# Moving layer 1's sums into step 7, beside the products of heads 0 to 3, and the maximum of head 5 ahead of the residual

## The chip, the cores and the metric

The kernel runs on one core of a Trainium2 chip. A core has five engines with their own instruction queues, each of which works strictly in order: PE multiplies matrices (its weight loads, PEld, overlap the products), DVE and ACT work on whole tiles, POOL works on tiles in SBUF and issues DMAs, and SP issues DMAs. PE writes its results to PSUM, a memory of eight banks, from where DVE and ACT read them. The metric is the time of one execution on the device in microseconds (us); lower is better.

## The reference, cut to what matters

Sixteen graphs of 1024 nodes with 256 features go through two layers, each with a norm ahead and a residual behind.

```python
# layer 0: attention with 8 heads of 32, masked by the graph
h = maximum(layernorm(x), 0)
Q, K, V = proj(Wq, bq), proj(Wk, bk), proj(Wv, bv)
scores = where(adj == 0, -inf, Q @ K.T * SCALE)
x = x + (softmax(scores) @ V) @ Wo.T + bo
# layer 1: edge scores from the features themselves
h = maximum(layernorm(x), 0)
e_k = leaky_relu((h * a_k) @ h.T, 0.2)        # one for each kind k = 1..4 of edge
scores = where(adj == k, e_k, -9e15)
x = x + softmax(scores) @ h
```

In these inputs adj holds only 0 and 1, so that one kind of edge occurs; a branch behind the loop handles the others and is not taken.

## The kernel before, in words

A tile is 128 nodes of a graph; there are 8 tiles to a graph and 128 in all. The main loop (L839) runs over s, one tile a round, and inside it over h = 0 to 7, which the text calls steps. The order of the instructions is written out by hand (`tc.manual_schedule()`, L787): each engine runs its share in the order of the source, and waits are put in where data or buffers require them. In one round several tiles are in work at different stages:

- `now` (class `Attend`) is the tile whose eight heads are scored. In step h PE makes `scores(h)` (L461), DVE takes the maximum and applies the mask (`softmax_max`, L473), and ACT does the exponential of the head before (`softmax_exp`, L490). The head before that is transposed: heads 0, 1, 4 and 5 by DVE in blocks that SP's DMAs then place (L381, L386), heads 2, 3, 6 and 7 by PE with copies by ACT (`turn_half`, L590, L591). Tile 7 of a graph has only heads 0 and 1 in blocks, tile 0 only heads 4 and 5; the others of heads 0, 1, 4 and 5 then go over PE with copies by DVE, and their exponentials write in another order.
- `now.combine(0)` (L526) multiplies heads 0 to 3 with the values in step 7; `was.combine(1)`, of the tile before, does heads 4 to 7 in step 3. `was.output()` (L541) writes y in step 4, `was.residual()` (L547) adds x on DVE in step 5, and `norms` (L182, L183, then POOL L167 to L172) takes the statistics of that and of the next piece.
- `piece` (class `Piece`) is a tile nine rounds ahead whose keys, queries and values are made: `normed` (ACT L223, step 4), `turn` (two PE transposes, L237, step 5), `turned` (two ACT copies, L249 and L250, step 5), `project(0, ...)` (k's projection, PE L267, step 6), `raised(0)` (ACT L309, step 7); in the next round, as `piece_was`, `project(1, ...)` in step 1, `values` in step 2, `raised(1)` (L309) in step 4.
- `edge` (class `Edges`) is a tile of layer 1, nine rounds behind: `score` in steps 0 and 2 (L627, L633), `softmax_max` in step 3 (L656), then `bend`, `leak` and, in step 6, `softmax_exp` (L680). In the next round, as `edge_was`, it is turned in blocks in step 0, and `gather(0)` and `gather(1)` (PE L698, 32 matmuls each) make its sums in steps 5 and 6. `store` (DVE L705, L707, and SP's output DMA L708) follows in step 6.

Rounds s = 0 to 9 have no gather, and rounds from s = 119 on have no `piece`.

Matmuls of combine and gather use a quarter of PE's columns each (128*32 in the profile), four side by side; all others use 128*128.

PSUM: `sides` hold the scores; of a tile in the middle, heads 4 and 6 and layer 1's edges have `sides[1]`, the others `sides[0]`. Two banks are cut in halves:

```python
banks = [ps_acc.tile([P, 2, D], F32, tag=f"acc{i}", name=f"acc{i}", bufs=1) for i in range(2)]
sums_place, brief, early, late = (banks[i // 2][:, i % 2, :] for i in range(4))
```

`sums_place` takes combine's products and layer 1's sums; `early` the projection of q; `late` the values, y, the piece's transposes and the projection of k, one after the other. All of them are called acc in the profile.

Behind the main loop the eight tiles of layer 1 of the last graph run by themselves; their sums alternate between `sums_place` and `late`.

Of the kernel before, what the change touches and what calls it, by code (L numbers as in the profile page):

```python
# [30 lines left out]
def by_blocks(t):  # L31
    return BY_BLOCKS.get(t, MIXED)
# [15 lines left out]
def gnn_kernel(  # L48
# [46 lines left out]
    sums_place, brief, early, late = (banks[i // 2][:, i % 2, :] for i in range(4))  # L95
# [92 lines left out]
    class Piece:  # L188
# [5 lines left out]
        def __init__(self, b, first, n=1):  # L194
            self.b, self.first, self.n = b, first, n
            self.cols = slice(first * P, (first + n) * P)
            self.projected, self.halved, self.queries = [], [], []
            self.tags = ("xin", "h0", "hT", "halves", "hTm") if n == 1 else ("pT", "pT", "pT", "p", "blocks")
# [158 lines left out]
    def load_key(b, h):  # L357
        kt = keys.tile([P, N], F32R, tag=f"k{h}", name=f"k{h}_{b}")
        c, r = divmod(h, GROUP)
        nc.sync.dma_start(  # L360
            out=kt.bitcast(F32),
            in_=kds[b][c, r * HD : (r + 1) * HD]
            .rearrange("d w n -> (d w) n").unsqueeze(1).to_broadcast([2 * HD, 2, N]),
        )
        keysets.setdefault(b, {})[h] = kt
# [228 lines left out]
    class Edges:  # L594


        def __init__(self, b, t, last=False):
            self.b, self.t, self.last = b, t, last
            self.rows = slice(t * P, (t + 1) * P)
            self.side = sides[t % 2 if last else 1]  # L600
            self.tags = {"sel": ("p", 4), "pT1": ("pT", 7)} if last else {}
            if last and t % 2:
                self.tags |= {"ha": ("hT", 1), "x1b": ("x1", 1), "h0": ("xb", 1)}
            self.sums = late if last and t % 2 else sums_place

        def buffer(self, tag, shape):
            tag, bufs = self.tags.get(tag, (tag, 1))
# [168 lines left out]
    def attend_of(s):  # L776
        return Attend(*divmod(s, NT)) if 0 <= s < B * NT else None

    def edges_of(s):
        s -= LAG  # L780
        return Edges(*divmod(s, NT), s >= (B - 1) * NT) if 0 <= s < B * NT else None

    def piece_of(s):
        s += LEAD
        return Piece(*divmod(s, NT)) if s < B * NT else None

    with tc.manual_schedule():  # L787
        first = [Piece(0, 0, 4), Piece(0, 4, 4)]
        piece_was, piece_next = Piece(1, 0), piece_of(0)
        now, nxt = attend_of(0), attend_of(1)  # L790
# [39 lines left out]
        piece, edge, edge_was = piece_next, None, None  # L830
# [8 lines left out]
        for s in range(B * NT + 1):  # L839
            b, t = divmod(s, NT)  # L840

            def load_keys(h, end):
                if t == NT - 1 and b + 1 < B and 2 * h + end in KEY_STEPS:
                    load_key(b + 1, KEY_STEPS.index(2 * h + end))
                if t == 0 and 0 < b < B and 2 * (HEADS + h) + end in KEY_STEPS:
                    load_key(b, KEY_STEPS.index(2 * (HEADS + h) + end))

            nxt2, edge_nxt, piece_nxt = attend_of(s + 2), edges_of(s + 1), piece_of(s + 1)
            for h in range(HEADS):
                ending, eh = (now, h - 1) if h >= 1 else (was, HEADS - 1)  # L850
                turning, th = (now, h - 2) if h >= 2 else (was, HEADS + h - 2)

                load_keys(h, 0)


                if now:
                    now.scores(h)
                if h == 0 and piece_was:
                    piece_was.halve(0)
                if s == 0 and h == 1:  # L860
                    first[1].values()
                if h == 3 and edge:
                    edge.softmax_max()
                if h == 5:
                    if was:
                        was.residual()
                    norms(was, piece_nxt)
                if h == 6 and edge_was:
                    edge_was.gather(1)
                if now:  # L870
                    now.softmax_max(h)
                if h == 6 and edge_was:
                    edge_was.store()


                if h == 1 and edge:
                    edge.keep(0)
                if h == 2 and gone:
                    gone.turned_normed()
                if ending:  # L880
                    ending.softmax_exp(eh)

                if h == 3 and was:
                    was.turned_reciprocals()
                if h == 3 and edge:
                    edge.bend()
                    edge.keep(1)


                if h == 3:  # L890
                    if was:
                        was.combine(1)
                    if piece_was:
                        piece_was.biased()
                    if was:
                        was.combined()
                if turning and th in by_blocks(turning.t):
                    turning.turn_blocks(th)
                    turning.place_blocks(th)
                elif turning:  # L900
                    turning.turn(th, 0)
                    turning.turn(th, 1)


                if h == 0:
                    if edge:
                        edge.score(0)
                    if gone:
                        gone.normed()
                    if edge_was:  # L910
                        edge_was.turn_blocks()
                        edge_was.place_blocks()
                if h == 1:
                    if gone:
                        gone.turn_normed()
                    if piece_was:
                        piece_was.project(1, 0)
                        piece_was.project(1, 1)
                    if was:
                        was.reciprocals()  # L920
                    if piece_nxt:
                        piece_nxt.load()
                if h == 2:
                    if edge:
                        edge.score(1)
                    if piece_was:
                        piece_was.values()
                    if was:
                        was.turn_reciprocals()
                        was.add_bias()  # L930
                if h == 3:
                    if nxt:
                        nxt.load_queries()
                    if edge:
                        edge.leak()
                    if edge_was:
                        edge_was.load_nodes()
                    if nxt:
                        nxt.flag()
                        nxt.mask()  # L940
                if h == 4:
                    if was:
                        was.output()
                    if piece_was:
                        piece_was.raised(1)
                        piece_was.halve(1)
                    if piece:
                        piece.normed()
                    if piece_was:
                        piece_was.write_queries()  # L950
                    if edge_nxt:
                        edge_nxt.prepare()
                    if nxt2:
                        nxt2.load()
                if h == 5:
                    if edge_was:
                        edge_was.gather(0)
                    if piece:
                        piece.turn()
                    if piece:  # L960
                        piece.turned()
                if h == 6:
                    if edge:
                        edge.softmax_exp()
                    if was:
                        was.keep()
                    if now:
                        now.load_nodes()
                    if piece:
                        piece.project(0, 0)  # L970
                        piece.project(0, 1)
                if h == 7:
                    if now:
                        now.combine(0)
                    if piece:
                        piece.raised(0)
                load_keys(h, 1)
            gone, was, now, nxt = was, now, nxt, nxt2
            edge_was, edge = edge, edge_nxt
            piece_was, piece = piece, piece_nxt  # L980
# [84 lines left out]
```

## Time and profile before

| what | before |
|---|---|
| median of three runs | 3070.12 us (3068.62 to 3073.23) |
| the profiled execution, its own time | 3076.4 us |
| its span in the profile | 3074.5 us |
| DVE busy, share of the span | 2515.6 us, 82% |
| ACT busy | 2654.5 us, 86% |
| POOL busy | 2177.6 us, 71% |
| gathers, PE L698 | 8192 matmuls of 382 ns, 496.9 us of PE's time |
| combines, PE L526 | 16384 matmuls of 275 ns, 533.4 us |
| scores, PE L461 | 2048 matmuls of 453 ns, 760.6 us |
| maxima, DVE L473 | 1024 of 1208 ns |
| exponentials, ACT L490 | 1024 of 1224 ns |

How to read the profile: the page gives the busy time of each engine and its share of the span. The list of waits says who stood idle, until whose instruction ended: total, times, longest. The view of windows gives, for a stretch of time, its length and then each engine's busy time. The timeline lists instructions in order of time: start, duration, engine, line, operation, output<-inputs, tile and count of merged instructions, and in brackets idle time ahead of them. Matmuls are pipelined: a group's duration reaches over the start of the next group, so the time between two starts is what the first costs PE.

### The profile page before, as it was taken

The numbers are of one execution on the slowest core, as the hardware profiler recorded it, in microseconds if no ns is written. First come the engines' busy times: TensorE is split into PE (matmuls) and PEld (weight loads), VectorE is DVE, ScalarE is ACT, GpSimd is POOL, SyncE is SP. The second block draws the span as 40 slices with busy tenths as digits, with TensorE's granted clock in tenths as the row PEclk, the third lists the DMA queues.
The fourth block names the chain that finished last, engine by engine and source line by source line (L and its number), as shares of the span: only waits on it lengthen the run. The fifth ranks groups of instructions, "written<-read, shape, count | busy, mean of one in ns | idle before, by whom it ended". The sixth has DMA issues, their size and how long they took to land. (4 is left out here: it accounts for less than half of the span.)

```text
span 3074.5 us, 96254 instructions
## 1 busy us (share of the span) xinstructions
PE 2965.6 (96%) x36722; PEld 2230.1 (73%) x36722; DVE 2515.6 (82%) x4453; ACT 2654.5 (86%) x5159; POOL 2177.6 (71%) x2999
## 2 busy tenths in 40 slices
PE   7889999999999999999999999999999999999998
PEld 5667777777777777777777777777777777776664
DVE  5878888888888888888888788888888888888885
ACT  5888888899898998889889888988989888898882
POOL 3657777777777777777777777777777777776542
PEclk9999999999999999999999999999999999999999
DMA  7766777877777786777777777787777777777653
GB/s 245 219 219 205 237 235 222 255 216 243 231 225 243 230 257 209 232 247 220 246 230 228 235 232 243 221 255 221 220 247 228 251 211 235 237 227 236 191 168 100
DMA packets 597828, 695.68 MB, mean 226 GB/s; under 512 B 63280, under 2 KB 528560, under 8 KB 597360
## 3 DMA queue, kind: packets, MB, share of 16 engines
q1 hardware_dynamic: 528288, 477.29, 51.9%
q0 software_dynamic: 66960, 210.04, 21.0%
q8 instruction: 295, 4.83, 0.7%
q10 hardware_dynamic: 2112, 2.10, 0.2%
q14 instruction: 173, 1.42, 0.1%
HBM read 252.98 MB, written 134.22 MB: 126 GB/s over the span
## 5 line engine op out<-in xcount | busy, mean ns | idle before, releaser
L473 DVE CUSTOM_DVE_ANT_0 p<-s,neg 128x1024 f32<-128x1024 f32 x1024 | 1236.2, 1208 | 220.7 <-PE s L461 185.1
L490 ACT ACTIVATE p<-p,nmx 128x1024 f32<-128x1024 f32 x1024 | 1249.4, 1224 | 132.5 <-DVE nmx L473 123.9
L461 PE MATMUL s<-k,qt 128*128 128x512 f32 x2048 | 760.6, 453 | 15.5 <-DVE nmx L473 4.3
L591 ACT COPY pT<-trp 128x512 f32<-128x512 f32 x1024 | 549.4, 590 | 95.3 <-PE trp L590 94.9
L590 PE MATMUL trp<-ident,p 128*128 128x128 f32 x4608 | 604.5, 274 | 4.7 <-ACT pT L591 1.5
L590 PEld LDWEIGHTS trp<-ident,p 128*128 128x128 f32 x4608 | 531.0, 140 | 104.0 <-ACT pT L591 10.8
L381 DVE STREAM_TRANSPOSE blocks<-p 128x1024 f32<-128x1024 f32 x456 | 564.5, 1238 | 12.3 <-ACT p L680 10.6
L526 PE MATMUL acc<-pT,v 128*32 128x128 f32 x16384 | 533.4, 275 | 41.8 <-ACT recT L520 30.0
L526 PEld LDWEIGHTS acc<-pT,v 128*32 128x32 f32 x16384 | 453.5, 110 | 153.0 <-ACT recT L520 85.0
L698 PE MATMUL acc<-h,pT 128*32 128x256 f32 x8192 | 496.9, 382 | 2.8 <-DVE h L707 1.7
L441 POOL TENSOR_SCALAR neg<-adj 128x1024 bf16<-128x1024 int32 x128 | 467.9, 3655 | 42.9 <-ACT neg L453 33.7
L461 PEld LDWEIGHTS s<-k,qt 128*128 128x128 f32 x2048 | 322.9, 191 | 106.3 <-issue 43.0
L698 PEld LDWEIGHTS acc<-h,pT 128*32 128x32 f32 x8192 | 241.8, 109 | 207.8 <-issue 65.6
L676 POOL TENSOR_TENSOR sel<-sel,less 128x1024 f32<-128x1024 f32 x120 | 286.8, 2390 | 68.9 <-ACT less L665 47.6
L633 PE MATMUL s<-h1T,ha 128*128 128x512 f32 (+2 forms) x744 | 272.8, 490 | 2.7 <-ACT h1T L569 1.6
L674 POOL TENSOR_SCALAR less<-top 128x1 f32<-128x1 f32 x120 | 31.9, 266 | 274.0 <-DVE top L656 273.9
L324 POOL DMA_DIRECT2D qd<-halves x240 | 177.5, 780 | 58.7 <-POOL halves L314 31.8
L490 ACT ACTIVATION_READ_ACCUMULATOR p<-p,nmx 128x1 f32 x1024 | 206.8, 202 | 0.0
L510 POOL COPY wide<-rec 128x256 f32<-128x256 f32 x128 | 53.8, 420 | 204.2 <-DVE rec L508 204.2
L330 POOL DMA_DIRECT2D kd<-halves x240 | 172.2, 766 | 35.5 <-POOL halves L314 35.4
L314 POOL TENSOR_TENSOR halves<-full,halves 128x256 fp32r<-128x256 f32 x240 | 176.8, 737 | 20.6
L633 PEld LDWEIGHTS s<-h1T,ha 128*128 128x128 f32 x744 | 126.7, 190 | 70.7 <-issue 45.0
(117 smaller groups left out, 4328.4 us busy)
## 6 DMA issues: line engine op xcount, KB each, us to landing
pT<-blocks SPq DMA_DIRECT2D x2304, 128.0 KB, 3.5
qt<-qd SPq DMA_DIRECT2D x128, 512.0 KB, 4.5
k<-kd SPq DMA_DIRECT2D x128, 512.0 KB, 7.3
adj<-in_adj POOLq DMA_DIRECT2D x127, 512.0 KB, 5.0
qd<-halves POOLq DMA_DIRECT2D x240, 256.0 KB, 2.7
kd<-halves POOLq DMA_DIRECT2D x240, 128.0 KB, 4.1
xb<-in_x POOLq DMA_DIRECT2D x128, 128.0 KB, 4.2
x1d<-x SPq DMA_DIRECT2D x128, 128.0 KB, 4.0
```

The costliest lines, as they stand in the source:

```text
L324: nc.gpsimd.dma_start(out=qds[self.b][self.first, oc].rearrange("p u w n -> p u (w n)"), in_=halves.unsqueeze(1).to_broadcast([P, 2, 2 * P]),)
L381: nc.vector.transpose(blocks.rearrange("p b j q -> p j b q"), p)
L441: nc.gpsimd.tensor_scalar(self.neg, self.adj, 0.0, MASKED, ALU.is_equal, ALU.mult)
L461: nc.tensor.matmul(self.ps[:, cols], lhsT=self.qt[:, h, :], rhs=keysets[self.b][h][:, cols], start=True, stop=True,)
L473: nc.vector.tensor_tensor_reduce(out=p, in0=sides[h in self.second], in1=self.neg, scale=-SCALE, scalar=FLOOR, op0=ALU.add, op1=ALU.min, a ...
L490: nc.scalar.activation(to, of, AF.Exp, bias=nmx, scale=-1.0, accum_out=self.sums[:, h : h + 1])
L526: nc.tensor.matmul(sums_place[r * HD : (r + 1) * HD, g * P : (g + 1) * P], lhsT=vs[self.b][:, j, place_of(h) : place_of(h) + HD], rhs=self ...
L590: nc.tensor.transpose(tr[:, j, :], p[:, jj * P : (jj + 1) * P], ident)
L591: copy(pT[:, half * 4 : half * 4 + 4, :], tr)
L633: nc.tensor.matmul(self.side[:, cols], lhsT=self.ha[:, c, :], rhs=h1T[:, c, cols], start=(c == 0), stop=(c == NC - 1),)
L676: nc.gpsimd.tensor_tensor(self.sel, self.sel, self.less, ALU.subtract)
L698: nc.tensor.matmul(self.sums[a * HD : (a + 1) * HD, :], lhsT=self.pT[:, j, a], rhs=h1s[self.b][:, j, :], start=(j == 0), stop=(j == NT - 1),)
```

## The change

In step 5 the maximum of head 5 stands ahead of `was.residual()` and `norms` in DVE's order. In step 6 `edge_was.gather(1)`, `store` and the projection of k are gone, in step 5 `gather(0)`. In step 7, behind `scores(7)` and the turning of head 5, now stand in this order: the projection of k, `gather(0)`, `gather(1)`, `store`, `combine(0)`, `raised(0)`. Layer 1's sums of all graphs but the last go to `early` in place of `sums_place`; those of the last graph stay where they were.

```diff
-            self.sums = late if last and t % 2 else sums_place
+            self.sums = (late if t % 2 else sums_place) if last else early
...
                 if h == 3 and edge:
                     edge.softmax_max()
+                if now:
+                    now.softmax_max(h)
                 if h == 5:
                     if was:
                         was.residual()
                     norms(was, piece_nxt)
-                if h == 6 and edge_was:
-                    edge_was.gather(1)
-                if now:
-                    now.softmax_max(h)
-                if h == 6 and edge_was:
-                    edge_was.store()
...
                 if h == 5:
-                    if edge_was:
-                        edge_was.gather(0)
                     if piece:
                         piece.turn()
                     if piece:
...
                     if now:
                         now.load_nodes()
+                if h == 7:
                     if piece:
                         piece.project(0, 0)
                         piece.project(0, 1)
-                if h == 7:
+                    if edge_was:
+                        edge_was.gather(0)
+                        edge_was.gather(1)
+                        edge_was.store()
                     if now:
                         now.combine(0)
                     if piece:
```

## The prediction

> **What bounds the kernel now.** I read the page first, then the waits of PE, then the busy time of one whole round (the loop body for one tile `now`, from `scores(4)` to the next `scores(4)`), then that round in order of time.
>
> ```profile
> PE 2965.6 (96%) x36722; PEld 2230.1 (73%) x36722; DVE 2515.6 (82%) x4453; ACT 2654.5 (86%) x5159; POOL 2177.6 (71%) x2999
> ```
>
> ```profile
> PE acc L526 <- ACT recT L520: 30.0, 43, 1.6
> PE acc L267 <- ACT hTm L250: 16.1, 10, 1.7
> ```
>
> ```profile
> 1571.04:1593.77 22.73, 22.73 (x288) 17.32 (x285) 19.41 (x34) 20.59 (x42) 17.53 (x25) 1.00 0.77 227
> ```
>
> PE is 96% busy, its longest wait adds up to only 30.0 us, and in the round from 1571.04 to 1593.77 (tile t = 2 into t = 3) it is busy for all 22.73 us (the second number). So PE sets the end, and a round costs what PE's queue costs. But DVE (19.41) and ACT (20.59) are close behind, in a strict order, so PE is full only because its own order has always something ready. That order is what the change touches. Steps 5 to 7 of that round, and what PE's neighbours do there:
>
> ```profile
> 1573.16 0.82 PE L461 MATMUL s<-k,qt 128*128 128x512 f32 x2
> 1573.81 1.04 PE L590 MATMUL trp<-ident,p 128*128 128x128 f32 x8
> 1574.78 1.93 PE L698 MATMUL acc<-h,pT 128*32 128x256 f32 x32
> 1576.64 0.44 PE L237 MATMUL acc<-ident,h 128*128 128x128 f32 x2
> 1576.84 0.71 PE L461 MATMUL s<-k,qt 128*128 128x512 f32 x2
> 1577.48 1.93 PE L698 MATMUL acc<-h,pT 128*32 128x256 f32 x32
> 1579.35 1.16 PE L267 MATMUL acc<-hT,wkT 128*128 128x128 f32 x8
> 1580.26 0.71 PE L461 MATMUL s<-k,qt 128*128 128x512 f32 x2
> 1580.90 1.95 PE L526 MATMUL acc<-pT,v 128*32 128x128 f32 x64
> 1582.78 0.73 PE L461 MATMUL s<-k,qt 128*128 128x512 f32 x2
> ```
>
> ```profile
> 1576.04 1.08 ACT L591 COPY pT<-trp 128x512 f32<-128x512 f32 x2
> ...
> 1577.12 0.38 ACT L249 COPY hT<-acc 128x256 f32<-128x256 f32 x1
> ...
> 1577.39 0.38 ACT L250 COPY hTm<-acc 128x256 f32<-128x256 f32 x1
> ```
>
> On PE: scores(5), transposes of head 3, gather(0), `piece.turn` (L237), scores(6), gather(1), k's projection (L267), scores(7), combine(0), scores(0) of the next round. A group costs PE the time to the start of the next group. The two gathers (1.86 and 1.87 us) stand where they fill PE while residual (DVE L547, 0.42 us from 1574.63) frees `late` and ACT copies `hT` and `hTm` out of it until 1577.77.
>
> **What the change removes on PE.** Gather and combine use 128*32 tiles, all around them 128*128. Entering such an island costs 0.07 to 0.10: eight transposes take 0.97 before gather(0) and 0.87 elsewhere (1571.61 to 1572.48), a score pair 0.64 instead of 0.57. Leaving costs about 0.1: the last gather matmul starts at 1576.33 (end less the 0.38 of one), a round of four takes 0.22, so its slot ends at 1576.55, and the next group starts at 1576.64. Three islands become one: two entries (0.17) and two exits (0.20) go, and the merged block is 1.86 + 1.87 + 1.88 - 0.20 = **5.41 us** from the first gather matmul to scores(0). The bound from below zero gain is 5.61 (no exit saved); I take 5.41, since the drain shows in the rows. No instruction is added or removed.
>
> **What it uncovers.** New PE order: scores(5), transposes of head 3, `piece.turn`, scores(6), scores(7), projection, block, scores(0). Two waits come up that gather(0) and gather(1) covered.
>
> *First, `piece.turn` writes `late`, which residual must have read.* The maximum of head 5 now stands ahead of residual on DVE: scores end at 1573.98, the maximum runs from 1574.02 and lets its successor start 1.15 later (as L473 does throughout), residual takes 0.42 from 1575.17 and ends at 1575.60. PE would be free at 1574.68; `piece.turn` starts at 1575.65, **0.97 us** idle. Then 0.20, scores(6) at 1575.85, scores(7) at 1576.42 (the maximum of head 5 is long there), PE free at 1576.99. Behind the waiting transposes stand both scores, but DVE is still in the norms (1.55 us after residual's start) until about 1576.8, so nobody else loses.
>
> *Second, the projection reads `hT`, and `late` must be copied out.* ACT runs without a gap from exp(3) through copies, `raised(1)`, `normed`, exp(4) and copies to `hTm`; none of it moves. It can only lose its wait for `piece.turn`: "ACT hT <- PE acc L237" is 12.1 us in 41 rounds. Against the first rounds, where the pair of copies is followed by `hTm`'s end 1.62 us after its start (141.83 to 143.45), this round could end 0.11 earlier, those of t = 0 and 1 0.41; over the rounds 0.23 on average. So `hTm` ends at 1577.54 on average instead of 1577.77, and PE waits about another 0.6 us.
>
> The trace has this case already. In the first ten rounds there is no layer 1, so no gather covers anything:
>
> ```profile
> 143.04 0.41 ACT L250 COPY hTm<-acc 128x256 f32<-128x256 f32 x1
> 143.50 1.16 PE L267 MATMUL acc<-hT,wkT 128*128 128x128 f32 x8 [1.65 <-ACT hTm L250]
> 144.41 0.70 PE L461 MATMUL s<-k,qt 128*128 128x512 f32 x2
> ```
>
> PE idles 1.65 us there; these are the 10 waits, 16.1 us, of the list above.
>
> **Sum of one round.** From the end of `hTm`: 0.05 to the projection, 0.91 for it (143.50 to 144.41, after a wait), 0.10 entry, 5.41 block = 6.47 to scores(0). Before it was 1582.78 - 1577.77 = 5.01. With `hTm` 0.23 earlier: 6.47 - 5.01 - 0.23 = **+1.23 us**; with 5.61 for the block +1.43, with the better exit of 0.13 each +1.17. From scores(0) on, every step keeps its order, PE is full again, so nothing gives the time back.
>
> *Tile t = 7 of each graph.* There heads 4 and 5 are turned on PE, head 5 right before the projection, and their exponentials are the 2.26 us kind:
>
> ```profile
> 1505.28 2.26 ACT L490 ACTIVATE p<-p,nmx 128x1024 f32<-128x1024 f32 x1
> ...
> 1511.57 0.73 PE L461 MATMUL s<-k,qt 128*128 128x512 f32 x2
> ```
>
> That exponential ends at 1507.54 and is bound by ACT's queue. After: 0.05, eight transposes 0.87, projection 0.81, entry 0.10, block 5.41 = 1514.78 instead of 1511.57, **+3.2 us** (scores(7) and gather(1) no longer fill the time).
>
> *Other edits.* `store` now reads `early` on DVE after the block's gathers, about 1.6 us ahead of scores(0), and `raised(0)` on ACT reads `late` in the same bank: 1574.63 for residual is 0.09 after `raised(1)` (1573.90 + 0.64) ended, though the two read different halves of that bank, so `raised(0)` will wait for `store`. ACT idles some 1.9 us, exp(7) behind it ends about 0.8 us after scores(0) starts; before it ended at 1583.58, also 0.8 after. Its next readers come later, so the cost is 0; without that cover up to 0.5 us a round. The Trainium skill, page "PSUM — Partial Sum Buffer", section "PSUM bank collisions raise a hardware error", says that two engines must be kept apart on one bank and quadrant even at other addresses, reads against reads included. It speaks against putting the sums beside `late`, and agrees with the 0.09; by it ACT must wait, without it ACT would go on at once, and both give PE the same sum here. The output DMA of `store` is issued about 1.7 us later against scores(0); behind it on SP stand the DMAs of layer 1's next tile, whose blocks DVE makes only after max(0). The x1 DMA and head 5's four placing DMAs now go ahead of it. POOL's norm runs at 1581.77, five us after its statistics, so their delay of half a us costs nothing.
>
> **Count.** Of 109 rounds with both a gather and a piece (s = 10 to 118), 13 have t = 7: 96 x 1.23 = 118, 13 x 3.2 = 42. The ten rounds without gather gain, since scores(7) now goes into the wait: from `hTm` to scores(0) 3.48 before, 0.05 + 0.91 + 0.10 + 1.88 = 2.94 after, -5. The nine last (no piece, no wait) gain some 0.4 each, -3. Sum +152, on the profiled execution's own 3076.4 us (span 3074.5) 3228; the median of the runs shown is 6.3 lower, so **3222 us**, 5% slower.
>
> **Rivals.**
> 1. *Faster: one island, waits covered elsewhere.* PE gains 0.37 plus 0.10 of the projection's slow start in 119 rounds: 3070 - 56 = 3014. For it stands that PE is the bound. The deciding point: scores(0) comes no later than before only if the projection starts by 1582.78 - 5.41 - 0.10 - 0.91 = 1576.36; PE is free for it only at 1576.99, even were `hTm` ready at once. Both waits would have to shrink to 0.4 us together.
> 2. *Only residual's wait stays,* ACT running earlier than its order lets me see: 1576.99 + 6.42 = 1583.41, +0.63 a round: 3070 + 69 = 3139.
> 3. *Typical rounds as forecast, t = 7 no worse than they:* 3222 - 13 x 2 = 3196.
> 4. *ACT's wait for `store` enters the chain* through exp(7) and the copies of head 6: +0.5 more in 109 rounds, 3277.
> 5. *No effect:* if the islands' gain met the waits, 3070.
>
> **Numbers.** Forecast with rival 3 beside it 0.78, rival 2 0.07, rival 4 0.07, faster 0.05, none 0.03. The range from 3139 to 3277 reaches to rivals 2 and 4. What a measurement of this kernel can tell from no change is about 0.2%: faster 0.05, same 0.03, slower 0.92.
>
> **What would show it.** After: PE's list with "L237 <- DVE x L547" about 100 times near 0.9 us and "L267 <- ACT hTm" over 100 times near 0.6; one block of 32 + 32 + 64 matmuls of about 5.4 us with no 128*128 group inside; t = 7 rounds 3 us longer; ACT's L309 of k waiting for DVE L707. I am wrong if PE stays full between scores(5) and scores(0), or if `hTm` ends over 1 us earlier after scores(5).

## The result, and the profile after

The changed kernel takes 3225.05 us (median of four runs, 3224.49 to 3227.04) against 3071.68 us for the kernel before in the same comparison: ratio 1.05, 95% interval 1.0482 to 1.0519. It is slower, by 153 us, where 152 was forecast. The profiled execution took 3224.54 us, its span is 3222.7 us.

The page's line of busy times, and PE's longest waits:

```profile
PE 2949.4 (92%) x36722; PEld 2276.3 (71%) x36722; DVE 2504.3 (78%) x4453; ACT 2639.8 (82%) x5159; POOL 2174.9 (67%) x2999
```

```profile
PE acc L237 <- DVE x L547: 104.1, 118, 1.0
PE acc L267 <- ACT hTm L250: 58.6, 106, 1.3
...
PE trp L590 <- ACT p L490: 16.8, 17, 1.5
PE trp L590 <- ACT pT L591: 16.6, 17, 1.8
```

PE does the same 36722 matmuls in 16 us less busy time, and yet its share falls from 96% to 92%: it now waits. The first entry is new, the second was 16.1 us. The transposes of the piece wait for residual in 118 rounds, 0.88 us each; k's projection waits for the copies out of `late` in 106 rounds, 0.55 us each. The last two belong to tile 7.

A round like the one shown before (same tile of another graph, `scores(4)` to `scores(4)`), first as a window, then PE's timeline from the turning of head 3 on:

```profile
1645.73:1669.78 24.05, 22.56 (x288) 17.68 (x285) 19.28 (x34) 20.45 (x42) 17.48 (x25) 1.00 0.74 214
```

```profile
1648.51 1.04 PE L590 MATMUL trp<-ident,p 128*128 128x128 f32 x8
1650.42 0.41 PE L237 MATMUL acc<-ident,h 128*128 128x128 f32 x2 [0.88 <-DVE x L547]
1650.59 1.18 PE L461 MATMUL s<-k,qt 128*128 128x512 f32 x4
1652.38 1.16 PE L267 MATMUL acc<-hT,wkT 128*128 128x128 f32 x8 [0.61 <-ACT hTm L250]
1653.47 3.66 PE L698 MATMUL acc<-h,pT 128*32 128x256 f32 x64
1656.94 1.93 PE L526 MATMUL acc<-pT,v 128*32 128x128 f32 x64
1658.80 0.73 PE L461 MATMUL s<-k,qt 128*128 128x512 f32 x2
```

The round takes 24.05 us where it took 22.73, with 288 matmuls in both; PE is busy for 22.56, so 1.49 us are gaps. They are the two brackets, 0.88 and 0.61. The pair of scores(6) and scores(7), merged into one line, stands between them. The gathers and combine(0) are one block, 1653.47 to 1658.80, with nothing of 128*128 inside.

From the first maximum of a tile to that of the next, as means over graphs 2 to 14: tiles 0 to 6 take 1.04, 1.05, 1.21, 1.35, 1.12, 1.06 and 1.39 us longer than before, tile 7 takes 27.48 us instead of 23.99. In tile 7 PE waits for ACT twice:

```profile
1573.78 1.14 PE L590 MATMUL trp<-ident,p 128*128 128x128 f32 x8 [0.96 <-ACT pT L591]
1574.68 0.71 PE L461 MATMUL s<-k,qt 128*128 128x512 f32 x2
1576.86 1.09 PE L590 MATMUL trp<-ident,p 128*128 128x128 f32 x8 [1.47 <-ACT p L490]
```

The first transposes (head 4) wait for a copy that frees their place in PSUM, the second (head 5) for the exponential of that head.

A smaller part of the loss is not in PE's order. In a row of the windows view the third number from the end is the clock that PE was granted, as a share of the full one. It is 1.00 in the rounds shown of both kernels, but not everywhere:

```profile
1375.21:1382.04 6.83, 6.09 (x31) 4.75 (x33) 4.07 (x7) 4.59 (x8) 4.50 (x9) 0.50 1.00 342
```

In the changed kernel eight of the rounds s = 10 to 118, six of tile 7 and two of tile 6, hold a stretch of 3.4 or 6.8 us at 0.50. Against the median round of the same tile they are 0.1 to 2.1 us longer, some 8 us in all. The kernel before has no such stretch in these rounds, but one in each of six of its first ten rounds, where the changed kernel has two. What brings them is not shown.

### The profile page after: what moved, and what is told of

The parts are those of the page before. It is cut to its first block, busy times and chain, and to the rows that moved or that the text cites. A ratio compares the mean times of both kernels' runs of the same rounds, so it can differ in the third digit from the quotient of the medians.

```text
span 3222.7 us, 95849 instructions
## 1 busy us (share of the span) xinstructions
PE 2949.4 (92%) x36722; PEld 2276.3 (71%) x36722; DVE 2504.3 (78%) x4453; ACT 2639.8 (82%) x5159; POOL 2174.9 (67%) x2999
## 5 line engine op out<-in xcount | busy, mean ns | idle before, releaser
L461 PE MATMUL s<-k,qt 128*128 128x512 f32 x2048 | 733.9, 448 | 14.7 <-DVE nmx L473 5.1
L590 PE MATMUL trp<-ident,p 128*128 128x128 f32 x4608 | 611.8, 276 | 35.2 <-ACT p L490 16.8
L590 PEld LDWEIGHTS trp<-ident,p 128*128 128x128 f32 x4608 | 534.6, 141 | 141.0 <-ACT pT L591 32.8
L526 PE MATMUL acc<-pT,v 128*32 128x128 f32 x16384 | 524.4, 274 | 32.1 <-ACT recT L520 30.6
L526 PEld LDWEIGHTS acc<-pT,v 128*32 128x32 f32 x16384 | 463.4, 110 | 115.6 <-ACT recT L520 85.5
L698 PE MATMUL acc<-h,pT 128*32 128x256 f32 x8192 | 475.4, 382 | 1.8 <-DMA pT<-blocks 1.0
L461 PEld LDWEIGHTS s<-k,qt 128*128 128x128 f32 x2048 | 330.7, 190 | 110.0 <-issue 39.4
L698 PEld LDWEIGHTS acc<-h,pT 128*32 128x32 f32 x8192 | 256.7, 110 | 180.7 <-issue 7.5
L309 ACT ACTIVATE full<-acc,bk_t 128x128 f32<-128x128 f32 x240 | 75.4, 366 | 263.9 <-DVE h L707 169.9
L490 ACT ACTIVATION_READ_ACCUMULATOR p<-p,nmx 128x1 f32 x1024 | 215.8, 211 | 0.0
L267 PE MATMUL acc<-hT,wkT 128*128 128x128 f32 x960 | 141.7, 292 | 58.6 <-ACT hTm L250 58.6
```

What stands on the lines that cost most here:

```text
L461: nc.tensor.matmul(self.ps[:, cols], lhsT=self.qt[:, h, :], rhs=keysets[self.b][h][:, cols], start=True, stop=True,)
L490: nc.scalar.activation(to, of, AF.Exp, bias=nmx, scale=-1.0, accum_out=self.sums[:, h : h + 1])
L526: nc.tensor.matmul(sums_place[r * HD : (r + 1) * HD, g * P : (g + 1) * P], lhsT=vs[self.b][:, j, place_of(h) : place_of(h) + HD], rhs=self ...
L590: nc.tensor.transpose(tr[:, j, :], p[:, jj * P : (jj + 1) * P], ident)
L698: nc.tensor.matmul(self.sums[a * HD : (a + 1) * HD, :], lhsT=self.pT[:, j, a], rhs=h1s[self.b][:, j, :], start=(j == 0), stop=(j == NT - 1),)
```

## The experiments

Theory U says that the loss is PE's waits that gather(0) and gather(1) had covered, less a gain from fewer switches between 128*128 and 128*32. The rivals: O, the new order on DVE costs by itself; B, the new place in the bank of `late` costs; L, the long stretch without scores starves DVE and ACT; S, each wait costs its own length. Ratios are to the kernel before, with 95% intervals. Where times are compared with the changed kernel or with another experiment, they come from different comparisons, in which the kernel before took 3070.18 to 3074.46 us; a few us between them mean nothing.

**1. The maximum of head 5 first, alone (on the kernel before).**

```diff
+                if now and h == 5:
+                    now.softmax_max(h)
                 if h == 5:
                     if was:
                         was.residual()
                     norms(was, piece_nxt)
...
-                if now:
+                if now and h != 5:
                     now.softmax_max(h)
```

> The kernel before with one edit: the maximum of head 5 ahead of residual and the norms. Theory U (PE waits that the gathers covered are uncovered): gather(0) still keeps PE busy until about 1.0 us after residual ends in its new place, so nothing waits: 3072 us, within 6. Rival O (the new order on DVE is itself the cost, piece.turn waits for residual wherever it stands): +0.9 us in 118 rounds, about 3175. Rivals B (early shares its bank with late) and L (a long stretch of PE without scores starves DVE and ACT) expect 3072 too, since neither is touched.

Measured 3071.19 us, ratio 1.0003 (0.9994 to 1.0013). The later residual costs nothing as long as gather(0) stands ahead of `piece.turn`; O falls. Only the rounds without a gather, s = 1 to 9, show the wait:

```profile
PE acc L237 <- DVE x L547: 7.9, 9, 0.9
```

There it costs nothing, since the later wait for `hTm` shrinks by nearly as much (from 16.1 to 9.4 us).

**2. Residual first again (on the changed kernel).**

```diff
-                if now:
-                    now.softmax_max(h)
                 if h == 5:
                     if was:
                         was.residual()
                     norms(was, piece_nxt)
+                if now:
+                    now.softmax_max(h)
```

> The changed kernel with residual and the norms ahead of the maximum of head 5 again. Theory U: PE's wait for residual falls from 0.9 to about 0.4 us, but scores(7) need the maximum of head 5, which now ends 1.55 us plus its own 1.2 later; PE then gets past scores(7) about 0.4 us after hTm is ready, so the round gets longer by 0.4: 3225 + 46 = 3270. Rival O (residual's wait of 104 us is the cost): it gets shorter by 0.5 us in 118 rounds or more, 3165 or below. B and L: 3225.

Measured 3246.78 us, ratio 1.057 (1.0552 to 1.0587): 22 us slower than the changed kernel, the side that U gave, half its size. PE's waits here:

```profile
PE s L461 <- DVE nmx L473: 149.9, 133, 1.4
PE acc L526 <- ACT recT L520: 30.5, 43, 1.6
PE acc L237 <- DVE x L547: 30.4, 82, 0.7
```

The wait for residual fell from 104.1 to 30.4 us, the one for `hTm` from 58.6 to 2.5, and one for the maximum of head 5 of 149.9 came up: scores(7) share `sides[0]` with it. So the third edit of the change is a help to the rest of it.

**3. The sums in their old place (on the changed kernel).**

```diff
-            self.sums = (late if t % 2 else sums_place) if last else early
+            self.sums = late if last and t % 2 else sums_place
```

> The changed kernel with layer 1's sums in sums_place as before, all moves kept. Theory U: combine(0) goes to the same half of the same bank and must wait for store: gathers' end, 0.1 to store, 0.48 for it, 0.06 back, against a start that overlaps the gathers' end: +0.8 us in 119 rounds, 3320. Rival B (the place beside late is the cost, through raised(0) that waits for store): ACT's waits of 170 and 83 us go, 3125 or so. L: 3225.

Measured 3350.96 us, ratio 1.0915 (1.0897 to 1.0933). U's side, by 31 us more than expected.

```profile
PE acc L526 <- DVE h L707: 79.6, 117, 1.9
```

This wait of PE is new: combine(0) waits for `store`. Those for residual (104.0 us) and for `hTm` (58.0) stay as in the changed kernel. From the first gather to combine(0) a typical round takes 0.8 us longer, as U expected; but combine(0) itself, coming after a wait, takes 2.09 us instead of 1.86, and the rounds from s = 119 on lose 2 us each. The new place is needed for the block. The two waits that make the loss are there without it, so as their cause B falls.

**4. The piece's transposes in `brief` (on the changed kernel).**

```diff
-                    tr = by_chunk(late)
+                    tr = by_chunk(brief)
```

> The changed kernel with the piece's two transposes written to brief (idle in steps 5 and 6) instead of late, so that PE need not wait for residual there. Theory U: the two waits stand one behind the other and the end of hTm is set by ACT's queue, not by the transposes; the first wait goes, the second grows by as much, and the time stays: 3215 to 3226. Rival S (the waits add up, each costs its own): the 104 us of the first wait are gained, 3121.

Measured 3195.65 us, ratio 1.0406 (1.0388 to 1.0423): 29 us less than the changed kernel, outside U's range and far from S.

```profile
PE acc L267 <- ACT hT L249: 105.3, 106, 1.0
...
PE acc L237 <- ACT h L223: 18.6, 70, 0.4
```

The first wait fell from 104.1 to 18.6 us (for `normed`), the second rose from 58.6 to 105.3: the waits stand one behind the other, as U has it, and S falls. The 29 us come from what I had overlooked: the releaser is now L249, not L250. The projection reads only `hT`. It had waited for the copy of `hTm` too because it writes over `late`, out of which both copies read; with the transposes in `brief` nothing holds it but `hT`. The copy of `hTm` starts 0.27 us after that of `hT`; 106 rounds of that are 29 us, and tiles 0 to 6 are each shorter by 0.26 to 0.28 us (median rounds).

**5. K's projection in step 6 again (on the changed kernel).**

```diff
                     if now:
                         now.load_nodes()
-                if h == 7:
                     if piece:
                         piece.project(0, 0)
                         piece.project(0, 1)
+                if h == 7:
                     if edge_was:
```

> The changed kernel with k's projection in step 6 again, ahead of scores(7). Theory U: the projection waits for hTm, and scores(7) now stand behind it instead of in the wait: +0.57 us in 96 rounds and in the ten first ones, while the rounds of t = 7 gain about 0.8 each, since there the projection gets out from behind head 5: 3225 + 55 + 5 - 10 = 3275. Rivals B and L: 3225.

Measured 3288.8 us, ratio 1.0697 (1.0677 to 1.0717).

```profile
PE acc L267 <- ACT hTm L250: 107.1, 106, 1.7
```

PE waits for `hTm` 107.1 us in place of 58.6: scores(7) are behind the wait, not in it. U's side, and 14 us more than its number. The excess goes with the clock: in this execution 24 of the rounds s = 10 to 118 hold a stretch of 3.4 us at half clock (0.50), each some 1.6 us longer for it, against eight rounds in the changed kernel. Among rounds without one, tiles 0 to 6 take 0.46 us more than in the changed kernel (0.57 expected), and tile 7 about 0.9 less (0.8 expected); without the clock U's number would be too high.

**6. Both gathers together in step 5 (on the kernel before).**

```diff
-                if h == 6 and edge_was:
-                    edge_was.gather(1)
...
                     if edge_was:
                         edge_was.gather(0)
+                        edge_was.gather(1)
```

> The kernel before with gather(1) right behind gather(0) in step 5, 64 matmuls in one stretch, all else as before. Theory U: both waits stay covered, but piece.turn starts 1.8 us later, which pushes hTm about 1.2 us and the projection 0.3 us: 3072 + 30 = 3100. Rival L (the long stretch is the cost): nearly the loss of the changed kernel, 3200.

Measured 3160.53 us, ratio 1.0277 (1.026 to 1.0295), 60 us above U's number, more than half way to L's. From DVE's and PE's timelines of one round:

```profile
1642.81 1.23 DVE L473 CUSTOM_DVE_ANT_0 p<-s,neg 128x1024 f32<-128x1024 f32 x1 [1.94 <-PE s L461]
```

```profile
1643.04 1.16 PE L267 MATMUL acc<-hT,wkT 128*128 128x128 f32 x8 [0.27 <-ACT hTm L250]
...
1647.22 0.73 PE L461 MATMUL s<-k,qt 128*128 128x512 f32 x2 [0.31 <-DVE nmx L473]
```

```profile
PEld acc L526 <- DVE h L707: 63.0, 103, 1.9
```

Here L is right in part. Scores(6) come behind the long stretch, DVE stands idle 1.94 us for them and has its whole work of steps 6 and 7 still to do. So `store` is late, and combine(0), whose place it reads in this kernel, waits for it with its weight loads (the last line; 2.7 us in 7 waits in the kernel before); then scores(0) wait for the last maximum. In the changed kernel the stretch comes behind scores(7), and DVE's idle time there (2.00 us ahead of the first maximum of the next round) keeps hardly anybody waiting: PE's waits for a maximum are 5.1 us in the whole execution. How the 60 us divide I did not follow up.

**7. One gather moved.** On the changed kernel: gather(0) back in step 5, residual first (the edit of experiment 2), sums in `brief`, `store` behind combine(0), and head 5 of tile 7 turned behind combine(0).

```diff
-            self.sums = (late if t % 2 else sums_place) if last else early
+            self.sums = (late if t % 2 else sums_place) if last else brief
...
-                elif turning:
+                elif turning and th != 5:
...
                 if h == 5:
+                    if edge_was:
+                        edge_was.gather(0)
...
                     if edge_was:
-                        edge_was.gather(0)
                         edge_was.gather(1)
-                        edge_was.store()
                     if now:
                         now.combine(0)
+                    if turning and th not in by_blocks(turning.t):
+                        turning.turn(th, 0)
+                        turning.turn(th, 1)
+                    if edge_was:
+                        edge_was.store()
```

> A version meant to keep the gain without the waits: gather(0) back in step 5 and residual first as before; k's projection, gather(1) and combine(0) in step 7; sums in brief, so that store can follow combine(0); tile 7's head 5 turned behind combine(0). Theory U: no new wait, one 128*32 island less, 0.2 to 0.25 us in 119 rounds: 3045. Rivals L and O: 3072 or above, as the block of step 7 is still 96 matmuls long.

Measured 3039.63 us, ratio 0.989 (0.9873 to 0.9908): faster than both kernels, within 6 us of U's number. Where the changed kernel waits 104.1 and 58.6 us for residual and `hTm`, no wait of PE for residual is listed here, and for `hTm` this:

```profile
PE acc L267 <- ACT hTm L250: 2.5, 2, 1.2
```

With gather(0) back as cover both waits go, and the kernel gains. A block of 96 matmuls in step 7 shows no cost by its length.

**8. Tile 7's head 5 turned behind combine(0) (on the changed kernel).**

```diff
-                elif turning:
+                elif turning and th != 5:
...
                         now.combine(0)
+                    if turning and th not in by_blocks(turning.t):
+                        turning.turn(th, 0)
+                        turning.turn(th, 1)
```

> The changed kernel with one edit: in tile 7 of each graph head 5 is turned on PE behind combine(0), not ahead of the projection. Theory U: these 13 rounds no longer wait for the exponential of head 5 and cost 1.2 us more than before instead of 3.4: 3225 - 28 = 3197. Without the theory (t = 7 is long for another cause): 3225.

Measured 3203.45 us, ratio 1.0417 (1.0399 to 1.0434): 22 us less. The wait for the exponential is no longer among PE's longest, the one for the place in PSUM (16.3 us) stayed. It may be what the missing 6 us are; this run does not take it away.

**9. The whole block kept, the projection behind it.** On the kernel of experiment 8:

```diff
-                    tr = by_chunk(late)
+                    tr = by_chunk(brief)
...
-                if h == 0 and piece_was:
+                if h == 1 and piece_was:
                     piece_was.halve(0)
...
                 if h == 0:
+                    if piece_was and s:
+                        piece_was.raised(0)
...
                 if h == 7:
-                    if piece:
-                        piece.project(0, 0)
-                        piece.project(0, 1)
...
                     if piece:
-                        piece.raised(0)
+                        piece.project(0, 0)
+                        piece.project(0, 1)
```

> All of the change kept (one block of 128 matmuls in step 7, sums in early, maximum of head 5 first), with what waits taken off PE's way: the piece's transposes in brief, k's projection behind combine(0), raised(0) and halve(0) one step later in the next round, tile 7's head 5 turned behind combine(0). Theory U: only a short wait for normed is left, 0.2 us a round, against 0.4 to 0.55 saved by two islands less: 3030, faster than the kernel before and level with the version that moves one gather. Rival L (the long block costs by itself): not below 3070.

Measured 3091.05 us, ratio 1.0059 (1.0042 to 1.0076). A miss by 61 us.

```profile
PE trp L590 <- ACT pT L591: 30.9, 30, 1.8
PE acc L267 <- DVE h L707: 28.1, 83, 0.6
...
PE acc L237 <- ACT h L223: 17.8, 68, 0.4
```

134 of the 153 us are back, but each cover taken away has another wait beneath it: the projection now waits for `store`, which reads the other half of its bank; the transposes of head 4 in tile 7 wait for their place; and `piece.turn` waits for `normed`. Tiles 2 to 6 are about level with the kernel before, tiles 7 and 0 remain 1.5 and 0.6 us longer; of the 30 waits of L590, 16 lie in tile 7 and the other 14 in tile 0, 0.4 us each there. The time is on L's side (3070 or more). Against L stands that PE's busy time is 51 us less than before (2914.2 us), as two islands less would have it, and its idle time 63 more (172.3), while the three waits shown add up to 77. But no run keeps the whole block and is free of these waits, so that the length of the whole block costs nothing by itself is not shown.

**10. One gather moved, and the maximum of head 5 first (on the kernel of experiment 7).**

```diff
+                if now:
+                    now.softmax_max(h)
                 if h == 5:
                     if was:
                         was.residual()
                     norms(was, piece_nxt)
-                if now:
-                    now.softmax_max(h)
```

> The version with one gather moved, with the maximum of head 5 ahead of residual as well. Theory U: gather(0) covers residual in its later place, and scores(7), which there waited 24.6 us in 34 rounds for that maximum, wait no more: 3040 - 20 = 3020. Rival O (the order on DVE costs): 3040 or more.

Measured 3032.37 us, ratio 0.9866 (0.9849 to 0.9882), the fastest version of the study. It gains 7 us on experiment 7, a third of the 20 expected, and the intervals of the two ratios overlap. PE's wait for the maximum went from 24.6 to 14.0 us, not to nothing. O, at 3040 or more, is not borne out.

**11. Both gathers ahead of the projection (on the changed kernel).**

```diff
-                    if piece:
-                        piece.project(0, 0)
-                        piece.project(0, 1)
                     if edge_was:
                         edge_was.gather(0)
                         edge_was.gather(1)
-                        edge_was.store()
+                    if piece:
+                        piece.project(0, 0)
+                        piece.project(0, 1)
+                    if edge_was:
+                        edge_was.store()
```

> The changed kernel with both gathers ahead of k's projection in step 7 (store behind the projection, all else kept). Theory U: the gathers run in the time in which PE waited for hTm, so that wait goes; one island more comes in; the wait for residual stays: some 0.4 us a round less than the changed kernel in 96 rounds, 3180. Rival S (waits do not matter, the place of the block does): 3225.

Measured 3237.97 us, ratio 1.0543 (1.0524 to 1.0561): slower than the changed kernel by 13 us, against both expectations.

```profile
1656.83 1.18 PE L461 MATMUL s<-k,qt 128*128 128x512 f32 x4
1658.64 3.66 PE L698 MATMUL acc<-h,pT 128*32 128x256 f32 x64 [0.64 <-ACT hTm L250]
```

The gathers read nothing of `hTm`, and yet they wait for it: they write `early`, and ACT's copies read `late` in the same bank. So in their new place they cannot cover that wait wherever they stand. That much of rival B is true, and U had left it out. PE's waits are about as long as in the changed kernel, so the 13 us are probably the island that comes in; it costs 0.13 us a typical round here, half of what experiment 12 finds for one. Why half is open.

**12. Three islands again (on the kernel of experiment 10).**

```diff
+                    if edge_was:
+                        edge_was.gather(1)
                     if piece:
                         piece.project(0, 0)
                         piece.project(0, 1)
-                    if edge_was:
-                        edge_was.gather(1)
                     if now:
                         now.combine(0)
```

> The version with one gather moved and the maximum of head 5 first, with k's projection between gather(1) and combine(0), so that PE has three 128*32 islands again. Theory U: nothing else waits, and the third island costs 0.2 to 0.28 us in 119 rounds: 3032 + 28 = 3060. If the switch of tiles costs nothing and the gain came from elsewhere: 3032.

Measured 3059.65 us, ratio 0.9964 (0.9951 to 0.9976): 27 us above experiment 10, as expected, with nearly the same list of PE's waits. The expectation counted 119 rounds, but from s = 119 on there is no projection to part gather(1) from combine(0), and the profile shows no loss there; the island is one more in 109 rounds. That is 0.25 us for one island of 128*32, entry and exit (0.28 by the two ratios), and in the profile tiles 0 to 6 are each 0.24 to 0.26 us longer (median rounds). The changed kernel has two islands less than the kernel before.

## Why the prediction was right, point by point

- *PE sets the end.* Right: the losses go with PE's waits, the gains with fewer islands; what is left over in experiment 5 goes with the clock.
- *The merged block, 5.41 us to scores(0).* 5.33 in the round shown. The projection took 1.09 to the first gather, not 0.91 + 0.10. The two errors cancel. The size of the gain, 0.37 us a round and 0.1 more at the projection, is borne out by experiment 12 (0.50 for two islands).
- *First wait, 0.97 us.* 0.88 in 118 rounds. Experiments 1 and 2 show its cause from both sides.
- *Second wait, about 0.6 us, since ACT's chain does not move.* 0.55 in 106 rounds. Experiment 4 shows that its end is fixed by ACT: with the first wait gone it grew. The two reasons given, that the projection reads `hT` and that `late` must be copied out, both hold, and experiment 4 parts them: without the second the wait ends 0.27 us earlier. The prediction priced them as one, to the end of the second copy, which is right here.
- *+1.23 us a typical round.* The mean of tiles 0 to 6 is 1.17, and 1.14 in the rounds s = 10 to 118 without a stretch at half clock.
- *Tile 7, +3.2 us.* 3.5 as a mean, 3.1 in the seven rounds with a `piece` and without a stretch at half clock. Experiment 8 shows that the exponential of head 5 makes about 1.6 of it. The wait of head 4's transposes for their place in PSUM was not seen; it lies under the longer one there, and came out in experiment 9.
- *Rounds without gather or piece, -8 us.* The first ten together took 8 us less, the rounds from s = 119 to 126 5 us less, -13 in all. So 96 x 1.17 + 13 x 3.5 - 13 = 145 us; the two spans differ by 148. How much of the 8 us is order is open, because six of these ten rounds held a stretch at half clock before and only two after.
- *152 us in all.* The mechanism is right; that the sum comes within 1 us is luck. The prediction has no term for the clock. For the rounds s = 10 to 118 it gives 160 us, and 160 were measured; but some 8 of them are the stretches at half clock, so that PE's order made about 150. And the two profiled executions differ by 148, the medians by 153.
- *`raised(0)` will wait for `store`, at no cost.* It does: ACT's L309 waits 169.9 us for DVE L707 in 65 rounds, and 83.1 in 40 more that the profile puts down to POOL (in the round shown `store` ends at 1657.68, L309 starts at 1657.80). ACT then still waits 0.45 us for PE ahead of the next copies, so it is not late. That it costs nothing is read from this row; no run took this wait away alone.
- *Rivals.* Faster would have needed both waits to shrink to 0.4 us together. Experiments 7 and 10 do it by leaving one gather where it covers them, and are faster. Of rival 4's condition, that ACT's wait for `store` enters the chain, the rows above show no sign.

## What to carry to other kernels

An engine that is always busy is held so by the order of its work: before an instruction is moved, look up what other engines do during it, for that is what the next instruction will wait for. Merge short islands of another tile shape, but leave behind what covers a transfer of results, and check which buffers share a bank, since in this program a write beside a result that is being read waits as if it wrote over it. Waits that stand one behind the other on one chain do not add up: to remove the first lengthens the second.

## What the runs showed of the hardware beyond that

A detour into 128*32 tiles and back costs PE 0.25 us beside the work it holds: 27 us in 109 rounds between experiments 12 and 10. The waits for a half of a bank that an instruction does not touch were 0.64 us in the round shown of experiment 11 (53.2 us in 96 rounds), and 28.1 us in 83 rounds in experiment 9; these waits are written into the program, and what the chip does without them was not tried. The granted clock fell to 0.50 for 3.4 or 6.8 us at a time in rounds that hold PE's waits: of the rounds s = 10 to 118, in eight of the changed kernel, in 24 of experiment 5 and in none of the kernel before. What brings it about was not tried.
